# The last pair's denominators inside its value products, and the router's product between output products

## The chip, the cores and the metric

The kernel runs on one core of one Trainium2 chip. Its time is the device time of one execution in microseconds; before the change it is 2727.31 us, the median of 3 runs (2726.57 to 2728.21).

## The reference

Four layers act in turn on x of shape (4, 512, 64, 64), all float32. What bears on the change is the first layer and how it hands over to the second. Cut to that:

```python
# layer 0: attention over the 4096 positions of an image, 64 channels
t = jnp.einsum('oc,bchw->bohw', w_qkv, x)            # key, query, value
scores = jnp.einsum('bdk,bdq->bkq', key_, query)
attn = jax.nn.softmax(scores, axis=1)                # over the keys k
out = jnp.einsum('bdk,bkq->bdq', value, attn)
out = jnp.einsum('oc,bchw->bohw', w_out, out)
x = scale * out + x
# layer 1: a convolution whose weights are a mixture of 8 experts, one mixture for each image
pooled = x.mean(axis=(2, 3))
rw = jax.nn.sigmoid(pooled @ router_w.T + router_b)
W = jnp.einsum('be,eoihw->boihw', rw, experts)       # for each of w1 (1x1), w2 (3x3), w3 (1x1)
...
```

So the weights of layer 1 can't be mixed before the mean of layer 0's whole output is known. Layer 2 is a linear attention, layer 3 a projection with two cumulative sums and a gate.

## The kernel before

The images go one after another through the four layers. The 4096 positions of an image are eight blocks of 512, held as four pairs of 1024 (`NPAIR` is 4); a pair of x is one SBUF tile of 128 x 4 x 1024.

**Layer 0.** For each pair of query blocks and each of 32 tiles of 128 keys, `scores` makes the product s of keys and queries (TensorE, L248), its exponential into a ring of 12 buffers (ScalarE, L251), and adds it into acc (VectorE, L256). `values` (L263) multiplies the ring's buffer with the values into av. Step i of 128 is tile i mod 32 of pair i // 32. The steps go in groups of six: scores of a group, then values of the group before (the loop of L324); the last two steps have a group of their own. Softmax is taken without the subtraction of a maximum, so its denominators are the column sums of acc: `sums` makes them with a product by ones (den, L279), inverts them (rec, L282, VectorE), and multiplies av by them (o, L286 or L288). `out_product` (L302) then makes the layer's output y in four parts m of 128 channels, and `add_out` (L307) adds it to x.

For pairs 0 and 1 all of that is hung into later groups of the loop through the list `late`. The last two pairs, 2 and 3, are treated otherwise, since the router waits for them. Only their sums over positions are needed for the mean, and these follow from o by a small product: `o` leaves its sum in osum, and `prod` (L370) adds osum times a matrix of 128 x 8 to what the earlier pairs gave. The product with ones (logit, L372) sums it over partitions. L374 to L377 make the sigmoid as 1 / (1 + exp(-z)), the exponential on ScalarE (L375). `own`, `part` and `sel` (L379 to L385) lay the eight mixing coefficients out as small matrices, so that TensorE can mix the experts: `mix` (L187). Pieces 0 to 3 (ex_0) are the weights of layer 1's first product, pieces 4 to 9 (ex_4, ex_7) are mixed likewise; pieces 10 to 12 (ex_10) are mixed on VectorE by `mix_by_expert` (L177 and L179, eight steps into wc).

**The order at the end of layer 0.** TensorE's instructions stay in the order of the program text (`manual_schedule` over the whole). Before the change that is: the scores of steps 126 and 127, the values of steps 120 to 127, den of pair 3, four output products of pair 2 (which ScalarE evicts into ring buffers 8 to 11, L367), two of pair 3, logit, one of pair 3, the first mix, the last of pair 3, the two other mixes, and then layer 1's first product c (`conv1`, L433). VectorE has the order of the text inside the `with` block of L363; what stands outside of it, as the steps of `mix_by_expert`, the scheduler puts where it sees room.

**Buffers.** Products of 128 x 2 x 512 (s, y, c) share three PSUM buffers (`pair_psum`), so each such product waits until the one three back has been read. av, den, logit and mix take turns in two single banks (`bank`). Of SBUF, `bigp` has three large buffers and `xpool` five: ex_4 is loaded where the keys were, ex_10 where ring buffers 0 to 3 were, ex_7 where ring buffers 4 to 7 (ringx) were, each when its last reader is through.

Of the kernel before, what the change touches and what calls it, by code (L numbers as in the profile page):

```python
# [20 lines left out]
KC = C // P  # L21
# [3 lines left out]
NPAIR = NBLK // 2  # L25
# [20 lines left out]
def unshifted(ctx: ExitStack, tc: tile.TileContext, fits, x, wqkv_t, wout_t, router_t,  # L46
# [3 lines left out]
    nc = tc.nc  # L50
# [9 lines left out]
    def pair_psum(name):  # L60
        return ps.tile([P, 2, NB], F32, tag="s", name=name, bufs=3)

    def bank(name, shape=(P, NB)):
        return ps.tile(list(shape), F32, tag="acc", name=name)
# [4 lines left out]
    def block(name, shape=(P, NB)):  # L69
        return blkp.tile(list(shape), F32, tag="blk", name=name)  # L70

    def flat(t):
        return t.rearrange("p h n -> p (h n)")
# [24 lines left out]
    def col(i, n=1):  # L98
        return prm_sb[:, i:i + n]
# [36 lines left out]
    groups = [(0, 1, G1, B1, M1, V1), (1, 1, G2, B2, M2, V2), (2, KC, G3, B3, M3, V3)]  # L136
# [15 lines left out]
    def router_of_values():  # L152


        wo_t = pair_psum("wo_t")
        wot_sb = block("wot_sb")
        for kc in range(KC):
            nc.tensor.transpose(wo_t[:, 0, kc * P:(kc + 1) * P], wout_sb[:, kc * P:(kc + 1) * P], ident)
        nc.vector.tensor_copy(wot_sb, wo_t[:, 0, :])
        for kc in range(KC):  # L160
            nc.tensor.matmul(wo_t[:, 1, 0:E], wot_sb[:, kc * P:(kc + 1) * P], router_sb[:, kc, :],
                             start=kc == 0, stop=kc == KC - 1)
        nc.vector.tensor_scalar(wr_sb, wo_t[:, 1, 0:E], col(SCALE), 1.0 / HW, ALU.mult, ALU.mult)
# [27 lines left out]
    def layer0(b, xs):  # L191
# [20 lines left out]
        def v_transpose(pr, vv, vsb):  # L212
            tr = vv[:, 1, :].rearrange("p (j c) -> p j c", c=P)
            for j in range(TPB):
                nc.tensor.transpose(tr[:, j, :], vsb[:, j * P:(j + 1) * P], ident)
            t0 = pr * 2 * TPB
            nc.vector.tensor_copy(
                vt[:, t0:t0 + 2 * TPB, :].rearrange("p (h j) d -> p j h d", h=2),
                tr.rearrange("p j (h d) -> p j h d", h=2))
# [21 lines left out]
        accs, avs = {}, {}  # L241

        def scores(i):
            pr, kt = divmod(i, NT)
            s = pair_psum(f"s_{b}_{i}")
            for h in range(2):
                r = slice(h * D, (h + 1) * D)
                nc.tensor.matmul(s[:, h, :], key[r, kt * P:(kt + 1) * P],  # L248
                                 qry[r, pr * NB:(pr + 1) * NB], start=True, stop=True)
            p = ring[i % RING]  # L250
            nc.scalar.activation(p, s, AF.Exp)  # L251
            if kt == 1:
                accs[pr] = four(f"acc_{b}_{pr}")
                nc.vector.tensor_tensor(accs[pr], ring[(i - 1) % RING], p, ALU.add)
            elif kt > 1:
                nc.vector.tensor_tensor(accs[pr], accs[pr], p, ALU.add)  # L256

        def values(i):
            pr, kt = divmod(i, NT)
            if kt == 0:  # L260
                avs[pr] = bank(f"av_{b}_{pr}")
            for h in range(2):
                nc.tensor.matmul(avs[pr][h * D:(h + 1) * D, :], vt[:, kt, :], ring[i % RING][:, h, :],  # L263
                                 start=kt == 0, stop=kt == NT - 1)
            if kt < NT - 1:
                return None
            if pr < NPAIR - 1:
                av = block(f"avsb_{b}_{pr}")
                nc.scalar.copy(av, avs[pr])
                avs[pr] = av  # L270
            return pr

        recs, outs = {}, {}

        def sums(pr, early=True):
            av, acc = avs[pr], accs[pr]
            den = bank(f"den_{b}_{pr}")
            for h in range(2):
                nc.tensor.matmul(den[h * D:(h + 1) * D, :], ones[:, 0:D], acc[:, h, :],  # L279
                                 start=True, stop=True)  # L280
            rec = block(f"rec_{b}_{pr}")
            nc.vector.reciprocal(rec, den)  # L282
            o = block(f"o_{b}_{pr}")
            if pr >= NPAIR - 2:
                i = pr - NPAIR + 2
                nc.vector.scalar_tensor_tensor(o, av, 1.0, rec, ALU.mult, ALU.mult, accum_out=osum[:, i:i + 1])  # L286
            else:
                nc.vector.tensor_tensor(o, av, rec, ALU.mult)  # L288
            recs[pr], outs[pr] = rec, o
            if early:  # L290
                sum_range(pr)

        def sum_range(pr):
            i = b * NPAIR + pr
            nc.vector.tensor_reduce(stat[:, 0, i:i + 1], recs[pr], AX.X, ALU.add)
            nc.vector.tensor_reduce(stat[:, 1, i:i + 1], recs[pr], AX.X, ALU.min)

        def out_product(pr, m):
            y = pair_psum(f"y_{b}_{pr}_{m}")
            for h in range(2):  # L300
                r = slice(h * D, (h + 1) * D)
                nc.tensor.matmul(y[:, h, :], wout_sb[r, m * P:(m + 1) * P], outs[pr][r, :],  # L302
                                 start=True, stop=True)
            return y
# [6 lines left out]
        def out_step(pr, m):  # L311
            add_out(pr, m, out_product(pr, m))
# [9 lines left out]
        groups = [range(i, min(i + RING // 2, NPAIR * NT)) for i in range(0, NPAIR * NT, RING // 2)]  # L322
        late = []
        for g, group in enumerate(groups):  # L324
            for i in group:
                scores(i)
            if g == 0:
                v_transpose(*pend)
                if b == 0:
                    router_of_values()  # L330
                continue
            for _ in range(2):
                if late and late[0][0] < g:
                    late.pop(0)[1]()
            for i in groups[g - 1]:
                pr = values(i)
                if pr is not None:
                    late.append((g, lambda pr=pr: sums(pr)))
                    if pr < NPAIR - 2:
                        late += [(g + 1, lambda pr=pr, m=m: out_step(pr, m)) for m in range(KC)]  # L340
# [15 lines left out]
        pr = NPAIR - 1  # L356
# [5 lines left out]
        ex10 = load_experts(b, 10, 3, bigp, "big", pack=False)  # L362
        with tc.manual_schedule(engines={mybir.EngineType.DVE}):  # L363
            sums(pr, early=False)
            for m in range(KC):
                y = out_product(pr - 1, m)
                nc.scalar.activation(ring[8 + m], y, AF.Copy, scale=col(SCALE))  # L367
            ys = [out_product(pr, m) for m in range(2)]
            prod = small.tile([P, E], F32, tag="prod", name=f"prod_{b}")
            nc.vector.scalar_tensor_tensor(prod, wr_sb, osum[:, 1:2], base, ALU.mult, ALU.add)  # L370
            logit = bank(f"logit_{b}", (P, E))
            nc.tensor.matmul(logit, ones, prod, start=True, stop=True)  # L372
            rw = small.tile([P, E], F32, tag="rw", name=f"rw_{b}")
            nc.vector.tensor_tensor(rw, logit, col(RB, E), ALU.add)  # L374
            nc.scalar.activation(rw, rw, AF.Exp, scale=-1.0)  # L375
            nc.vector.tensor_scalar(rw, rw, 1.0, None, ALU.add)
            nc.vector.reciprocal(rw, rw)  # L377
            own = small.tile([P, 2, 4], F32, tag="own", name=f"own_{b}", bufs=1)
            nc.vector.tensor_tensor(own, rw.rearrange("p (g e) -> p g e", g=2),  # L379
                                    which[:, None, :].to_broadcast([P, 2, 4]), ALU.mult)  # L380
            part = small.tile([P, 2], F32, tag="part", name=f"part_{b}", bufs=1)
            nc.vector.tensor_reduce(part, own, AX.X, ALU.add)
            sel = small.tile([P, 2, 32], F32, tag="sel", name=f"sel_{b}", bufs=1)
            for g in range(2):
                nc.vector.tensor_scalar(sel[:, g, :], row, part[:, g:g + 1], None, ALU.mult)  # L385
            ys.append(out_product(pr, 2))
            add_out(pr, 0, ys[0])
            mix(wcq, sel, ex0)
            ys.append(out_product(pr, 3))
            for m in range(1, KC):  # L390
                add_out(pr, m, ys[m])
            for m in range(KC):
                xm = xs[pr - 1][:, m, :]
                nc.vector.tensor_tensor(xm, xm, flat(ring[8 + m]), ALU.add)
            sum_range(pr)
# [960 lines left out]
```

## Time and profile before

| Quantity | Value |
|---|---|
| time, median of 3 | 2727.31 us |
| span of the profiled execution | 2725.2 us |
| TensorE busy | 2668.1 us, 98% |
| VectorE busy | 1960.1 us, 72% |
| ScalarE busy | 1306.8 us, 48% |
| granted TensorE clock, mean | 0.997 |
| HBM traffic | 42 GB/s over the span |
| reciprocal rec of 128 x 512 | 3.35 us, 16 times |
| eviction of y by ScalarE (L367), 128 x 1024 | 1.115 us, 16 times |
| mixing step on VectorE (L179), 128 x 384 | 0.617 us, 28 times |

Busy times are unions of an engine's instructions; since matmuls overlap, a busy TensorE need not be at its peak. In the lines of groups and of the timeline, "out<-in" names tiles without their numbers, "xN" is how many instructions were merged, and a bracket gives the idle time of the engine before the instruction and what ended it. In the view of waits a line has who waited, for whom, the total in us, how often, and the longest.

### The profile page before, as it was taken

The numbers are of one execution on the slowest core, as the hardware profiler recorded it, in microseconds if no ns is written. First come the engines' busy times: TensorE is split into PE (matmuls) and PEld (weight loads), VectorE is DVE, ScalarE is ACT, GpSimd is POOL, SyncE is SP. The second block draws the span as 40 slices with busy tenths as digits, with TensorE's granted clock in tenths as the row PEclk, the third lists the DMA queues.
The fourth block names the chain that finished last, engine by engine and source line by source line (L and its number), as shares of the span: only waits on it lengthen the run. The fifth ranks groups of instructions, "written<-read, shape, count | busy, mean of one in ns | idle before, by whom it ended". The sixth has DMA issues, their size and how long they took to land.

```text
span 2725.2 us, 25637 instructions
## 1 busy us (share of the span) xinstructions
PE 2668.1 (98%) x10046; PEld 1112.3 (41%) x10046; DVE 1960.1 (72%) x2197; ACT 1306.8 (48%) x1483; POOL 10.8 (0%) x26
## 2 busy tenths in 40 slices
PE   8999999999999999999999999999999999999998
PEld 3333364344333345444433334544443333554443
DVE  2688766787468776678747777667874787866787
ACT  4545354445555535345555553525554545352545
POOL 1000000000000000000000000000000000000000
PEclk9999999999999999999999999999999999999999
DMA  5000210021200020002220002001121000200011
GB/s 188 1 1 0 101 31 1 16 108 76 80 1 1 1 101 31 1 24 100 77 78 1 1 1 101 32 0 62 62 113 42 1 1 4 98 31 1 31 46 48
DMA packets 34545, 115.15 MB, mean 42 GB/s; under 512 B 2928, under 2 KB 12144, under 8 KB 32880
## 3 DMA queue, kind: packets, MB, share of 16 engines
q1 hardware_dynamic: 34416, 113.43, 11.2%
q8 instruction: 81, 1.33, 0.2%
q14 instruction: 48, 0.39, 0.0%
HBM read 79.86 MB, written 33.55 MB: 42 GB/s over the span
## 4 chain that ended last, share of the span: by engine, by line
PE 86%; DVE 8%; ACT 3%; DMA 1%; issue 1%; SPq 1%; DVEq 0%; ACTq 0%
PE s L248 17%; PE av L263 17%; PE sx L758 14%; PE zy L758 11%; PE c L433 4%; PE kq L209 4%; PE c L482 3%; PE z L532 2%; PE c L505 2%; PE wv L676 2%; PE vv L209 2%; PE g L594 2%; PE xtr L577 2%; PE y L302 2%; PE c2e L482 2%
## 5 line engine op out<-in xcount | busy, mean ns | idle before, releaser
L248 PE MATMUL s<-qv,key 64*128 64x512 f32 x2048 | 468.9, 602 | 1.8 <-ACT ring L251 1.8
L256 DVE TENSOR_TENSOR acc<-acc,ring 128x1024 f32<-128x1024 f32 x312 | 381.7, 1223 | 101.0 <-ACT ring L251 72.0
L251 ACT ACTIVATE ring<-s 128x1024 f32<-128x1024 f32 x336 | 317.6, 1037 | 223.9 <-PE s L248 223.9
L263 PE MATMUL av<-ring,qv 128*64 128x512 f32 x1344 | 304.5, 595 | 0.0
L248 PEld LDWEIGHTS s<-qv,key 64*128 64x128 f32 x2048 | 188.9, 187 | 275.1 <-issue 172.1
L256 DVE TENSOR_TENSOR acc<-acc,ringx 128x1024 f32<-128x1024 f32 x168 | 205.5, 1223 | 101.7 <-ACT ringx L251 89.5
L251 ACT ACTIVATE ringx<-s 128x1024 f32<-128x1024 f32 x176 | 172.1, 1039 | 207.0 <-PE s L248 207.0
L758 PE MATMUL sx<-t,sx 128*128 128x512 f32 x512 | 236.8, 596 | 0.0
L263 PEld LDWEIGHTS av<-ring,qv 128*64 128x64 f32 x1344 | 93.2, 137 | 198.7 <-issue 198.7
L263 PE MATMUL av<-ringx,qv 128*64 128x512 f32 x704 | 167.1, 597 | 0.0
L763 ACT COPY zy<-sx 128x512 f32<-128x512 f32 x64 | 36.5, 570 | 240.1 <-PE sx L758 230.6
L808 DVE TENSOR_TENSOR_SCAN t<-sx,t 128x512 f32<-128x512 f32 x128 | 148.8, 1210 | 1.7
L758 PEld LDWEIGHTS sx<-t,sx 128*128 128x128 f32 x512 | 95.6, 190 | 128.0 <-issue 121.3
L797 ACT COPY t<-s 128x1024 f32<-128x1024 f32 x64 | 127.1, 1992 | 40.6 <-DVE s L791 40.6
L767 ACT ACTIVATE e<-sx,prm_sb 128x512 f32<-128x512 f32 x128 | 87.0, 686 | 123.8 <-PE sx L758 123.8
L791 DVE TENSOR_TENSOR_SCAN s<-wc,s 128x512 f32<-128x512 f32 x128 | 146.1, 1204 | 0.0
L814 ACT ACTIVATE s<-t 128x1024 f32<-128x1024 f32 x64 | 125.5, 1987 | 1.0 <-DVE t L808 0.9
L758 PE MATMUL sx<-t,wq 128*128 128x512 f32 x256 | 117.0, 597 | 7.5 <-ACT e L767 7.5
L209 PE MATMUL kq<-x,wqkv_sb 128*64 128x512 f32 x512 | 115.9, 605 | 7.2 <-DMA x<-in_x_dram 6.2
L758 PE MATMUL zy<-t,wq 128*128 128x512 f32 x256 | 118.6, 604 | 2.5 <-ACT zy L763 2.5
L758 PE MATMUL zy<-x,wq 128*128 128x512 f32 x256 | 116.2, 594 | 0.0
L758 PE MATMUL sx<-x,wq 128*128 128x512 f32 x256 | 116.1, 594 | 0.0
(195 smaller groups left out, 3388.5 us busy)
## 6 DMA issues: line engine op xcount, KB each, us to landing
out_dram<-s SPq DMA_DIRECT2D x64, 512.0 KB, 2.6
x<-in_x_dram SPq DMA_DIRECT2D x15, 2048.0 KB, 8.6
ex<-in_packed_dram SPq DMA_DIRECT2D x8, 1536.0 KB, 7.1
ex<-in_packed_dram SPq DMA_DIRECT2D x4, 2048.0 KB, 8.0
ex<-in_experts_dram SPq DMA_DIRECT2D x4, 2048.0 KB, 7.8
wq<-in_wproj_t_dram SPq DMA_DIRECT2D x32, 256.0 KB, 4.8
ex<-in_experts_dram SPq DMA_DIRECT2D x4, 1536.0 KB, 6.7
x<-in_x_dram SPq DMA_DIRECT2D x4, 512.0 KB, 6.8
```

What stands on the lines that cost most here:

```text
L209: nc.tensor.matmul(y[h * D:(h + 1) * D, :], wqkv_sb[:, kc, col0:col0 + D], xs[pr][:, kc, h * NB:(h + 1) * NB], start=kc == 0, stop=kc == K ...
L248: nc.tensor.matmul(s[:, h, :], key[r, kt * P:(kt + 1) * P], qry[r, pr * NB:(pr + 1) * NB], start=True, stop=True)
L251: nc.scalar.activation(p, s, AF.Exp)
L256: nc.vector.tensor_tensor(accs[pr], accs[pr], p, ALU.add)
L263: nc.tensor.matmul(avs[pr][h * D:(h + 1) * D, :], vt[:, kt, :], ring[i % RING][:, h, :], start=kt == 0, stop=kt == NT - 1)
L433: nc.tensor.matmul(y[:, h, :], wc[:, kc, :], xs[pr][:, kc, h * NB:(h + 1) * NB], start=kc == 0, stop=kc == KC - 1)
L482: nc.tensor.matmul(y[:, lo - a:hi - a], u, v[:, lo:hi], start=dy == 1, stop=dy == 2)
L758: nc.tensor.matmul(y, w[:, c, self.kind, self.j * P:(self.j + 1) * P], v[:, c, :], start=c == 0 and k in (1, 5), stop=c == 1, skip_group_c ...
L791: nc.vector.tensor_tensor_scan(self.half(i, h), along[:, self.j + 2 * i, :], self.half(i, h), 0.0, ALU.mult, ALU.add)
L797: nc.scalar.copy(self.t[i].rearrange("p (w r) -> p w r", w=W), self.s[i].rearrange("p (r w) -> p w r", w=W))
L808: nc.vector.tensor_tensor_scan(th, down[:, i, :], th, 0.0, ALU.mult, ALU.add)
L814: nc.scalar.activation(self.s[i].rearrange("p (r w) -> p w r", w=W), tw, AF.Sigmoid)
```

## The change

Two things are moved, in each of the four images; no operation is added or taken away.

- The denominators of the last pair: den and the reciprocal become a function of their own, `inverse_sums`. For the last pair it is called in the midst of the value products, ahead of step 124, when the scores of all 128 steps have been issued. `sums` then only multiplies av by the inverse.
- The router's product: of the four output products of pair 2, two stand ahead of `prod` and logit; the two others, and the first three of pair 3, stand behind `sel` in the text. Before, all four of pair 2 and two of pair 3 stood ahead of logit.

The aim is that the chain from the last values to the mixing coefficients has its long reciprocal beside the value products, and that TensorE has output products to make while the coefficients are worked out.

```diff
-        def sums(pr, early=True):
-            av, acc = avs[pr], accs[pr]
+        def inverse_sums(pr):
+            acc = accs[pr]
             den = bank(f"den_{b}_{pr}")
             for h in range(2):
                 nc.tensor.matmul(den[h * D:(h + 1) * D, :], ones[:, 0:D], acc[:, h, :],
                                  start=True, stop=True)
-            rec = block(f"rec_{b}_{pr}")
-            nc.vector.reciprocal(rec, den)
+            recs[pr] = block(f"rec_{b}_{pr}")
+            nc.vector.reciprocal(recs[pr], den)
+
+        def sums(pr, early=True):
+            if early:
+                inverse_sums(pr)
+            av, rec = avs[pr], recs[pr]
             o = block(f"o_{b}_{pr}")
...
-            for i in groups[g - 1]:
+            for n, i in enumerate(groups[g - 1]):
+                if g == len(groups) - 1 and n == 4:
+                    inverse_sums(NPAIR - 1)
                 pr = values(i)
...
             sums(pr, early=False)
-            for m in range(KC):
+            def out_before(m):
                 y = out_product(pr - 1, m)
                 nc.scalar.activation(ring[8 + m], y, AF.Copy, scale=col(SCALE))
-            ys = [out_product(pr, m) for m in range(2)]
+
+            for m in range(2):
+                out_before(m)
             prod = small.tile([P, E], F32, tag="prod", name=f"prod_{b}")
...
-            ys.append(out_product(pr, 2))
+            for m in range(2, KC):
+                out_before(m)
+            ys = [out_product(pr, m) for m in range(3)]
             add_out(pr, 0, ys[0])
             mix(wcq, sel, ex0)
             ys.append(out_product(pr, 3))
```

More of the change, by code (lines that the diff above doesn't have):

```diff
@@ L288, in sums @@
                 nc.vector.tensor_tensor(o, av, rec, ALU.mult)
-            recs[pr], outs[pr] = rec, o
+            outs[pr] = o
             if early:
```

## The prediction

> **What bounds the kernel now.** I read the page first: parts 1 and 4 say which engine sets the span.
>
> ```profile
> PE 2668.1 (98%) x10046; PEld 1112.3 (41%) x10046; DVE 1960.1 (72%) x2197; ACT 1306.8 (48%) x1483; POOL 10.8 (0%) x26
> ...
> PE 86%; DVE 8%; ACT 3%; DMA 1%; issue 1%; SPq 1%; DVEq 0%; ACTq 0%
> ```
>
> TensorE is busy nearly always, so only two things can shorten the span: fewer matmuls, or fewer moments in which TensorE stands. The change has the same matmuls, so I asked the view of waits for TensorE alone, and kept the two lines of the stretch that is edited:
>
> ```profile
> PE mix L187 <- DVE sel L385: 5.7, 4, 1.4
> ...
> PE y L302 <- ACT ring L367: 2.6, 4, 0.7
> ```
>
> Once per image TensorE stands 1.4 us before the first mix and 0.65 us before the second pair's worth of output products: 8.3 us of 2725. This is all that can be had. Third, the timeline of image 0 around that stretch, engine by engine (start, length, then what; a pair of matmul records is issued every 0.43 us, the lengths overlap):
>
> ```profile
> 291.51 3.65 PE L263 MATMUL av<-ring,qv 128*64 128x512 f32 x16
> 295.00 3.60 PE L263 MATMUL av<-ringx,qv 128*64 128x512 f32 x16
> 298.43 1.03 PE L279 MATMUL den<-acc,ones 128*64 128x512 f32 x4
> 299.39 3.70 PE L302 MATMUL y<-o,wout_sb 64*128 64x512 f32 x16
> 303.74 1.99 PE L302 MATMUL y<-o,wout_sb 64*128 64x512 f32 x8 [0.65 <-ACT ring L367]
> 305.66 0.39 PE L372 MATMUL logit<-prod,ones 128*128 128x8 f32 x2
> 305.98 1.13 PE L302 MATMUL y<-o,wout_sb 64*128 64x512 f32 x4
> 308.52 1.92 PE L187 MATMUL mix<-ex,sel 128*32 128x512 f32 x16 [1.41 <-DVE sel L385]
> 310.38 1.13 PE L302 MATMUL y<-o,wout_sb 64*128 64x512 f32 x4
> 311.43 2.79 PE L187 MATMUL mix<-ex,sel 128*32 128x384 f32 x32
> ```
>
> ```profile
> 291.83 2.55 DVE L256 TENSOR_TENSOR acc<-acc,ringx 128x1024 f32<-128x1024 f32 x2 [2.78 <-ACT ringx L251]
> ...
> 299.50 3.36 DVE L282 RECIPROCAL rec<-den 128x512 f32<-128x512 f32 x1 [5.12 <-PE den L279]
> ...
> 302.90 0.69 DVE L286 SCALAR_TENSOR_TENSOR o<-av,rec 128x512 f32<-128x512 f32 x1
> ...
> 303.63 0.23 DVE L370 SCALAR_TENSOR_TENSOR prod<-wr_sb,osum,base 128x8 f32<-128x8 f32 x1
> ...
> 306.09 0.17 DVE L374 TENSOR_TENSOR rw<-logit,prm_sb 128x8 f32<-128x8 f32 x1 [2.23 <-PE logit L372]
> 306.29 0.21 ACT L375 ACTIVATE rw<-rw 128x8 f32<-128x8 f32 x1 [1.59 <-DVE rw L374]
> ...
> 308.23 0.38 DVE L385 TENSOR_SCALAR sel<-row,part 128x32 f32<-128x32 f32 x2
> ...
> 308.52 4.86 DVE L307 SCALAR_TENSOR_TENSOR x<-y,prm_sb,x 128x1024 f32<-128x1024 f32 x4
> ```
>
> See two things. The sum of exponentials is complete at 294.38 (291.83 + 2.55), yet its product den runs at 298.43, behind all the value products; VectorE sits 5.12 us before the 3.36 us reciprocal. And the chain reciprocal, o, prod, logit, rw, sel, mix is serial, with logit queued behind two output products. In issue times TensorE loses a little more than the idle column says: the last pair of y issues at 302.50, so the next could at 302.92, and does at 303.74 (0.82); the product before the mix ends issuing at 306.94, the mix could at 307.04 and does at 308.52 (1.48). Together 2.30 us an image. The next layer's first matmul (c, L433) starts at 314.15. The stretch repeats in the other images within 0.1 us.
>
> [...] So whatever stands behind a waiting matmul waits with it, which the two stalls above show. [...] The exponential of the router will now stand between Copy evictions; the compiled program has no table load there, and in the trace the evictions (1.11 us long) start 1.00 us apart, an overlap of 0.11. [...] dependent wc steps of 0.62 us start 0.65 us apart.
>
> **Part 1: den and its reciprocal in the midst of the values.** It stands before the fifth of the last eight value steps, at 295.00, and takes 0.86 us there instead of at 298.43: same matmuls, same 128*64 shape, so no cost on TensorE. It adds a wait in front of four value steps: for the last acc, done at 294.38, 0.6 us early, in every image (2.87 us after the first of the eight steps, against 3.49). So nothing. The reciprocal starts when den has drained: 295.00 + 0.43 + 0.59 + 0.05 = 296.07, ends 299.43. It lies in VectorE's 5.12 us of idleness. The values now end where den ended, at 299.46. Hence o from 299.50 to 300.20 and prod to 300.47: 3.4 us earlier than before. One buffer, ringx, is read until 0.86 us later, so the load of ex_7 is issued at about 299.5 instead of 298.64; it took 8.9 us, lands at 308.4 and is needed by the third mix at 311: hidden.
>
> **Part 2: logit after two output products.** Output products start at 299.39 as before; two of them take until 301.21, a change of shape 0.13, logit 301.33 to 301.72 (its 0.32 us of TensorE is only moved). rw at 301.93. The exponential stands behind the second eviction on ScalarE, which starts at 301.57, so it starts one interval later, 302.57, and ends 302.78. Queued behind it are evictions three and four; the third starts at 302.82 instead of 302.57, the fourth ends at about 304.93. Before, sel started 1.74 us after the exponential's end (306.50 to 308.23), so it now starts at 304.51 and is complete at 304.90. TensorE meanwhile: six more products of 0.86 us and two changes of shape, 301.65 to 306.04; mix could start at 306.14. Their buffers: y needs its predecessor three back evicted, at 301.68, 302.68, 303.93, 304.93 for products due at 302.61, 303.47, 304.33, 305.19. All in time. So both old stalls, 2.30 us, vanish.
>
> **Part 3: what the order makes of it.** The compiled order of VectorE differs in one thing that the diff does not show: after sel, four of the mixing steps of wc (L179, of ex_10) now stand ahead of the first addition x<-y (L307), which used to follow sel at once. The steps are 0.65 us apart: 304.81 + 4 x 0.65 = 307.4, a little earlier for the overlap of the last, 307.30. The addition takes 1.28: 308.58. It frees the buffer that the fourth output product of the last pair needs, which stands behind the mix on TensorE: the mix takes 1.85 and would let it start at 307.99, so it waits until about 308.65. That is a new wait of 0.65 us, and everything behind it (second and third mix, layer 1) waits with it. From there to c it is 3.78 us as before: c at 312.4 instead of 314.15, a gain of 1.7 us.
>
> In image 0, ex_10 landed at 303.60, and the first wc step, which stands ahead of sel in VectorE's queue, would start at 303.34. So 0.3 is lost: 1.4. In the other images it landed 10.1 to 10.7 us after the first of the eight value steps against 11.8 needed.
>
> **Does it last?** The same wc steps are absent later, so VectorE has less to do in layer 1. ScalarE now makes the sums of taps ahead of the first h, and its second part waits for VectorE's taps, at about 320.7; h then ends at about 323.2, as before (323.26), and the taps are done. VectorE stood 1.80 us before the third pair's sums, waiting for h of TensorE's product: it is paced by TensorE and moves with it. c of layer 1 itself needs none of this: it ran 27.66 us without a gap. Later transfers are released by buffers that move too.
>
> Sum: 1.4 + 3 x 1.7 = 6.5 us; 2727.3 - 6.5 = 2720.8.
>
> **The rivals.** (B) The new wait is not there, because the steps of wc overlap more or the mix takes longer: 4 x 2.30 = 9.2, 2718.1. For it: the wait is only 0.65 us, the difference of two long sums. Against: the 0.65 us spacing is measured between dependent steps. (C) The chain to the first addition is later. It has no slack: each us is lost whole. If ex_10 lands 1 us later than I take it in every image, the gain is 0.7 to 0.9: some 3.3 us, 2724.0. For it: the landing spread from 10.1 to 12.1 us. Against: three of four were early by 1.1 us or more. (D) Slower: the taps ahead of h on ScalarE, or den waiting for acc, hold TensorE for longer than was gained, say 1.6 us net an image: 2727.3 + 6.4 = 2733.7. Against: layer 1's transformed products start at 341.89, while VectorE had the sums they need by 335.2, 6.7 us of room.
>
> **How the numbers follow.** My forecast 0.64, B 0.12, C 0.17, D 0.07. The bound of 0.2% is 5.45 us; the forecast of 6.5 lies only 1 us over it, so of its 0.64 I put 0.57 above; with B and a third of C, faster 0.75. The rest of the forecast and of C: same 0.19. Slower 0.06. The range takes in B at one end and C at the other: 2717.4 to 2724.0, outside of it D and the tails.
>
> **What would show it.** Right: TensorE's waits have no line of mix behind sel and none of y behind ring; y behind x of L307 appears, about 0.65 us, four times; den directly between two groups of av; rec's wait ends near 296.1; logit near 301.3; c starts 20.9 us after the first of the eight value steps, before 22.6. Wrong: a wait of av or den for acc; mix still waiting for sel; a wait of more than 1.5 us before the fourth product; a new gap before c of L482.

## The result, and the profile after

Of six runs each, the changed kernel takes 2718.76 us in the median (2717.71 to 2720.21) and the kernel before 2726.94 (2725.30 to 2728.21). The ratio is 0.9970, its 95% interval 0.9957 to 0.9983: faster by 8.2 us, and by 4.6 to 11.7 at the ends of the interval. The forecast was 6.5 us faster (2720.8), inside that interval. The span of the profiled execution went from 2725.2 to 2717.1 us at the same mean granted clock, 0.997. Line numbers from here on are those of the changed kernel; the numbers that moved and matter are y L307 (302 before), addition L312 (307), logit L381 (372), sel L394 (385), c L444 (433). L405 is the additions of pair 2, whose products were evicted to the ring.

The page of the kernel after, parts 1 and 4, engine shares:

```profile
PE 2667.3 (98%) x10046; PEld 1114.7 (41%) x10046; DVE 1961.2 (72%) x2197; ACT 1306.6 (48%) x1483; POOL 10.7 (0%) x26
...
PE 86%; DVE 9%; ACT 2%; DMA 1%; issue 1%; SPq 1%; DVEq 0%; ACTq 0%
```

The same matmuls keep TensorE busy for as long as before, to within 1 us; the bound is unchanged. The gain has to be in waits. The view of waits for TensorE alone, after (who waited, for whom, us in total, times, longest):

```profile
PE zy L769 <- ACT zy L774: 2.5, 4, 0.7
PE y L307 <- DVE x L312: 2.4, 4, 0.6
PE s L248 <- ACT ring L251: 1.8, 8, 0.2
```

The two lines of before, mix behind sel (5.7 us) and y behind ring (2.6), are not in the list at all. (What held y in the second of them was not the ring; see the experiment den_early_only.) One has come: y behind the addition x, four times 0.6. The neighbours are shown because they stand for what has not changed. In this view TensorE has 8.3 us less of the old and 2.4 us more of the new, 5.9 net; in issue times, as the forecast counts, it is more, as the offsets below show. TensorE's timeline of image 0, after (start, length, engine, line, what, how many; brackets as before):

```profile
291.49 3.65 PE L263 MATMUL av<-ring,qv 128*64 128x512 f32 x16
294.98 1.03 PE L279 MATMUL den<-acc,ones 128*64 128x512 f32 x4
295.84 3.60 PE L263 MATMUL av<-ringx,qv 128*64 128x512 f32 x16
299.37 1.99 PE L307 MATMUL y<-o,wout_sb 64*128 64x512 f32 x8
301.29 0.39 PE L381 MATMUL logit<-prod,ones 128*128 128x8 f32 x2
301.61 4.56 PE L307 MATMUL y<-o,wout_sb 64*128 64x512 f32 x20
306.10 1.93 PE L187 MATMUL mix<-ex,sel 128*32 128x512 f32 x16
308.62 1.13 PE L307 MATMUL y<-o,wout_sb 64*128 64x512 f32 x4 [0.60 <-DVE x L312]
309.68 2.79 PE L187 MATMUL mix<-ex,sel 128*32 128x384 f32 x32
312.40 4.13 PE L444 MATMUL c<-x,wc 128*128 128x512 f32 x9
```

From 291.49 to 306.10 there is no bracket: den, logit and five output products run one behind the other. The one bracket left is 0.60 us, before the fourth product of the last pair. VectorE's timeline of the same stretch says why:

```profile
291.81 2.56 DVE L256 TENSOR_TENSOR acc<-acc,ringx 128x1024 f32<-128x1024 f32 x2 [2.78 <-ACT ringx L251]
296.06 3.36 DVE L282 RECIPROCAL rec<-den 128x512 f32<-128x512 f32 x1 [1.69 <-PE den L279]
299.52 0.69 DVE L291 SCALAR_TENSOR_TENSOR o<-av,rec 128x512 f32<-128x512 f32 x1
...
304.50 0.38 DVE L394 TENSOR_SCALAR sel<-row,part 128x32 f32<-128x32 f32 x2
304.80 2.58 DVE L179 SCALAR_TENSOR_TENSOR wc<-ex,rw,wc 128x384 f32<-128x384 f32 x4
307.29 1.28 DVE L312 SCALAR_TENSOR_TENSOR x<-y,prm_sb,x 128x1024 f32<-128x1024 f32 x1
```

The reciprocal starts at 296.06 and ends at 299.42, 0.10 us before o needs it: it is as long as before, but now runs beside the value products. Behind sel stand the four mixing steps, and only then, at 307.29, the first addition; it ends at 308.57, and the fourth product starts 0.05 later.

To compare kernels I measured, in every image, when each operation starts after the first of the last eight value steps (291.49 above). These are differences of timeline entries, image 0, in us; "last y" is the fourth output product of the last pair:

| kernel | den | rec | logit | sel | first mix | first addition | last y | c |
|---|---|---|---|---|---|---|---|---|
| before | 6.92 | 7.99 | 14.15 | 16.72 | 17.01 | 17.01 | 18.87 | 22.64 |
| after | 3.48 | 4.56 | 9.79 | 13.01 | 14.60 | 15.79 | 17.12 | 20.90 |
| den_early_only | 3.48 | 4.56 | 13.29 | 15.86 | 16.15 | 16.15 | 18.00 | 21.78 |
| router_early_only | 6.92 | 7.99 | 12.49 | 15.03 | 18.97 | 18.47 | 20.83 | 24.60 |
| den_two_steps_earlier | 2.92 | 4.05 | 11.00 | 14.22 | 15.81 | 17.00 | 18.33 | 22.11 |
| add_before_mixing | 3.48 | 4.56 | 9.79 | 12.14 | 14.60 | 13.01 | 16.46 | 20.23 |

c after is 20.90 in all four images and was 22.64: 1.74 us an image, 6.96 in all. That is the part of the 8.2 us whose cause is in sight. The other 1.1 us of the spans is smaller than the spread of runs of one kernel (2.5 us among the six above), and no stretch shows it in all four images: some 0.75 us of it lie in layer 2, where TensorE waits on work that VectorE has behind the landing of the weights wq (image 3 gains 1.0 us there, image 1 loses 0.7), and 0.4 between the end of layer 2 of image 2 and layer 0 of image 3.

### The profile page after: what moved, and what is told of

The parts are those of the page before. It is cut to its first block, busy times and chain, and to the rows that moved or that the text cites. A ratio compares the mean times of both kernels' runs of the same rounds, so it can differ in the third digit from the quotient of the medians.

```text
span 2717.1 us, 25649 instructions
## 1 busy us (share of the span) xinstructions
PE 2667.3 (98%) x10046; PEld 1114.7 (41%) x10046; DVE 1961.2 (72%) x2197; ACT 1306.6 (48%) x1483; POOL 10.7 (0%) x26
## 4 chain that ended last, share of the span: by engine, by line
PE 86%; DVE 9%; ACT 2%; DMA 1%; issue 1%; SPq 1%; DVEq 0%; ACTq 0%
PE s L248 17%; PE av L263 17%; PE sx L769 14%; PE zy L769 11%; PE c L444 4%; PE kq L209 4%; PE c L493 3%; PE c L516 2%; PE z L543 2%; PE wv L687 2%; PE vv L209 2%; PE g L605 2%; PE xtr L588 2%; PE c2e L493 2%; PE y L307 1%
```

## The experiments

Theory: each half of the change does one thing. The early denominators take the reciprocal off the serial chain; the early logit lets output products fill the time of the sigmoid. The early logit is of no use alone, since it waits for the reciprocal unless that is early too; the early denominators alone leave the wait of the mix as it was. What is not gained is the 0.6 us of the new wait, and its cause is the order of VectorE, not the number of its instructions. The rival: one half gives all of it, and the other is idle. Each kernel is compared with the kernel before on the same chip (medians 2726.33 us for the first four, 2726.03 for the last four).

**The change once more (again).** No edit.

> The changed kernel unaltered, a second profile. Theory (two old stalls of 2.30 us an image removed, one new wait of 0.6 us): layer 1's first product c starts 20.90 us after the first of the last eight value steps in all four images, to 0.05 us; the 1.1 us by which the first profile gained more than 4 x 1.74 us is the landing of the projection weights wq in layer 2, which varies from 9.1 to 10.2 us after the last transformed product from one execution to the next, so its sum over the images will differ again and the time will be 2717.7 to 2720.2. Rival (the change itself makes layer 2 shorter): the sum of the landings stays 0.7 us or more under that of before.

2718.85 us (2716.44 to 2720.68), ratio 0.9971 (0.9959 to 0.9983): 7.5 us faster. c came 20.90 us after the first value step, 20.93 in image 1; the new wait is 2.4 us in all again. So the gain is 8.2 and 7.5 us in the two measurements, of which 7.0 lie in the stretch. Of the theory on the rest, one half held: it is not the change. The addition sx, which waits for the landing of wq, starts 41.22 us after the last transformed product of layer 1 in the kernel before, added over the images, 40.47 in the first profile of the changed kernel and 40.98 here, so the rival's 0.7 us did not come back. But the landing is not the whole of the rest either: here 1.2 us of it lie ahead of the stretch of image 0 (the first value step at 290.34 instead of 291.51), in work that the change does not touch.

**Denominators early, logit where it was (den_early_only).**

```diff
-            for m in range(2):
+            for m in range(KC):
                 out_before(m)
+            ys = [out_product(pr, m) for m in range(2)]
...
-            for m in range(2, KC):
-                out_before(m)
-            ys = [out_product(pr, m) for m in range(3)]
+            ys.append(out_product(pr, 2))
```

> Only the denominators and the reciprocal of the last pair are moved; logit stands behind six output products, as before. Theory (one serial chain; each part needs the other): the wait of y goes, logit at 13.3 us after the first of the last eight value steps, sel 2.9 later, the wait of mix for sel stays at 1.4 us of idle TensorE; c at 21.75, against 22.64 before: 0.9 us an image, 3.6 in all, 2723.3. Rival 1 (the early reciprocal is the whole gain): c at 20.9, 2719. Rival 2 (it gives nothing alone): 2727.

2722.60 us, ratio 0.9985 (0.9979 to 0.9992): 3.7 faster, by the table 4 x (22.64 - 21.78) = 3.4. The waits of TensorE in this kernel:

```profile
PE kq L209 <- DMA x<-in_x_dram: 5.9, 1, 5.9
PE mix L187 <- DVE sel L395: 5.7, 4, 1.4
PE xtr L587 <- ACT pos L551: 4.3, 4, 1.1
```

Mix waits for sel for exactly as long as before the change, 5.7 us: that wait goes only when logit is moved as well. The early reciprocal alone removes the other, which the view of before put down to the ring. Here six output products run without a gap:

```profile
298.84 5.48 PE L307 MATMUL y<-o,wout_sb 64*128 64x512 f32 x24
```

The fifth, the first of the last pair, starts at 302.38, when the second eviction into the ring has ended (302.14) but the third has not (303.14); so it needs only the second. In the kernel before, the second ended at 302.68, and the fifth product came only at 303.74. It multiplies o of the last pair, which was complete at 303.60; that the third eviction ended at 303.69, close by, is why the view names the ring. What ended last was o, and o waits for the reciprocal.

**Logit early, denominators where they were (router_early_only).**

```diff
             for n, i in enumerate(groups[g - 1]):
-                if g == len(groups) - 1 and n == 4:
-                    inverse_sums(NPAIR - 1)
...
+            inverse_sums(pr)
             sums(pr, early=False)
```

> Only the router's product is moved; den and its reciprocal stand behind all value products, as before. Theory: logit waits for prod at 12.4 us after the first of the last eight value steps, while output products due at 9.8 stand behind it, so TensorE stands 2.6 us there; the wait for sel goes; VectorE has five steps of wc ahead of the first addition, so the last output product waits 0.7 us; c at 23.6, against 22.64 before: 1.0 us an image lost, 4 in all, 2731. Rival (the order of the router's product is a gain by itself, the 1.4 us of the mix): c at 21.2, 2721.

2734.22 us, ratio 1.0027 (1.0016 to 1.0038): 7.9 slower, and slower than expected. TensorE's timeline of image 0:

```profile
299.54 1.99 PE L307 MATMUL y<-o,wout_sb 64*128 64x512 f32 x8
304.16 0.36 PE L380 MATMUL logit<-prod,ones 128*128 128x8 f32 x2 [2.63 <-DVE prod L378]
304.45 6.26 PE L307 MATMUL y<-o,wout_sb 64*128 64x512 f32 x20
310.64 1.92 PE L187 MATMUL mix<-ex,sel 128*32 128x512 f32 x16
```

The 2.63 us wait is what the theory asks for: the queue stands behind logit, logit behind prod, prod behind the reciprocal. What was not expected is the line below. The same twenty matmuls took 4.56 us after the change and take 6.26 here, with no bracket. The view of windows of this kernel has the granted clock (the columns after the window and its length are the busy times of PE, PEld, DVE, ACT and POOL, then PEclk, DMA share, GB/s):

```profile
302.00:304.00 2.00, 0.00 (x0) 0.00 (x0) 1.93 (x4) 0.84 (x1) 0.00 (x0) 1.00 0.83 307
304.00:306.00 2.00, 1.84 (x8) 1.13 (x10) 1.11 (x6) 0.34 (x2) 0.00 (x0) 0.81 0.75 320
306.00:308.00 2.00, 2.00 (x6) 0.68 (x4) 1.96 (x7) 1.41 (x2) 0.00 (x0) 0.50 0.05 18
308.00:310.00 2.00, 2.00 (x10) 0.93 (x8) 1.90 (x4) 0.69 (x1) 0.00 (x0) 0.83 0.00 0
```

After the wait the clock is halved for a while: from 306 to 308 it is 0.50, and six matmul records of y fall there; the kernel after has twelve of them in two microseconds (304 to 306). The forecast of c was 23.6; it came at 24.60. The slow clock cost 1.70 us (6.26 against 4.56), but spared the last y its wait for x, which the forecast had at 0.7 us: the slowed queue came to that product after the addition was done. In image 3 the mix came 20.38 us after the first value step rather than 18.97, and c 26.01. So the wait of 2.63 us cost TensorE more than its length; den_first and router_after_three follow this up.

**The first addition ahead of the mixing steps (add_before_mixing).** The steps of `mix_by_expert` are written inside the fixed order, behind the additions of three of the four products.

```diff
-            for m in range(1, KC):
+            for m in range(1, KC - 1):
                 add_out(pr, m, ys[m])
+            mix_by_expert(wcq, rw, ex10)
+            add_out(pr, KC - 1, ys[KC - 1])
...
-        mix_by_expert(wc, rw, ex10)
```

> Both parts of the change, and the eight mixing steps of wc on VectorE fixed behind three of the four additions, so that the first addition follows sel at once. Theory (the new wait is the buffer of the last output product, held until the first addition): the wait of y for x goes, no other takes its place, c at 20.30 us after the first of the last eight value steps, 0.6 us an image and 2.4 in all faster than the changed kernel: 2716.4. Rival (another wait stands right behind, in the mixes or in layer 1, as the taps come later on VectorE): c at 20.9 or a new gap before layer 1's transformed products, 2718.8.

2717.91 us (2715.55 to 2718.78), ratio 0.9966 (0.9952 to 0.9980). VectorE of image 0, which begins 0.95 us earlier in this execution:

```profile
302.68 0.39 DVE L394 TENSOR_SCALAR sel<-row,part 128x32 f32<-128x32 f32 x2
303.54 3.67 DVE L312 SCALAR_TENSOR_TENSOR x<-y,prm_sb,x 128x1024 f32<-128x1024 f32 x3 [0.47 <-PE y L307]
307.12 0.60 DVE L177 TENSOR_SCALAR wc<-ex,rw 128x384 f32<-128x384 f32 x1
```

The addition now follows sel, the wait of y for x is gone from TensorE's list, and c comes at 20.23: 0.67 us an image, as expected (20.30). That shows the cause of the new wait. Over the whole kernel 2.7 us should follow; the median is 0.9 us under that of the change run beside it and the intervals overlap, so the gain is shown in the stretch, not in the time. In these two profiles layer 2 takes 0.9 us of it back, between the last transformed product and the transposes ktr (87.5 us over the images against 86.6); see the last experiment.

**Denominators two value steps earlier (den_two_steps_earlier).**

```diff
-                if g == len(groups) - 1 and n == 4:
+                if g == len(groups) - 1 and n == 2:
```

> The changed kernel with den and the reciprocal ahead of step 122 instead of 124. Theory (the place has 0.6 us of slack before acc is complete): den is due 1.72 us after the first of the last eight value steps and acc is complete at 2.9, so TensorE stands 1.2 us there, which nothing repays, since o waits for the last value step anyway; c at 22.1 instead of 20.90, 1.2 us an image and 4.8 in all slower than the changed kernel, 2723.6; the granted clock stays at 1.00, as with the 1.4 us stalls of before. Rival (a waiting den costs nothing, value steps are worked meanwhile): c at 20.9.

2723.84 us, ratio 0.9992 (0.9985 to 0.9998): 2.2 faster than the kernel before, and 5.0 slower than the changed kernel (4.8 expected). TensorE of image 0:

```profile
290.67 1.94 PE L263 MATMUL av<-ring,qv 128*64 128x512 f32 x8
293.60 1.08 PE L279 MATMUL den<-acc,ones 128*64 128x512 f32 x4 [0.99 <-DVE acc L256]
294.51 1.89 PE L263 MATMUL av<-ring,qv 128*64 128x512 f32 x8
```

Den is due two value steps, 1.7 us, earlier than in the change, but it starts only 0.56 us earlier (2.92 in place of 3.48), since acc is complete no sooner. TensorE is idle for 0.99 us, and six value steps stand behind it. Those 0.56 us are the slack of the forecast, measured from the other side. c is at 22.11, 1.21 us later, so the rival (a waiting den costs nothing) falls.

**Denominators ahead of all the last values (den_first).** As the last, with `n == 0`, four value steps ahead of where the change has it.

> The changed kernel with den and the reciprocal ahead of the first of the eight value steps. TensorE stands about 2.85 us in one piece. Theory A (a stall of 2.6 us or more lowers the granted clock to a half for some microseconds, as in the run with the router's product alone moved): granted clock 0.5 within the 5 us behind the stall, value steps spaced 0.85 us instead of 0.43 for a while, c at 25.4 or later, 2737 or more. Theory B (that slowness came from the output products themselves or the transfers beside them): clock 1.00, c at 23.8, 2730.5.

2734.76 us, ratio 1.0030 (1.0017 to 1.0042): 8.7 slower. TensorE waits for acc 11.4 us in all, 2.85 an image, and in three of four images the clock is halved behind it. The time lies between the forecasts of theory A (2737 or more) and theory B (2730.5). Two windows of image 0; the stall ends at 294.56, inside the first:

```profile
293.00:295.00 2.00, 0.44 (x2) 0.20 (x4) 1.41 (x2) 0.00 (x0) 0.00 (x0) 1.00 0.76 301
295.00:297.00 2.00, 2.00 (x8) 0.72 (x6) 0.82 (x1) 0.00 (x0) 0.00 (x0) 0.50 0.96 412
```

The clock of 0.50 came here behind a stall at another place, ahead of value products, so it is not made by the output products. Nor is it made by the transfers beside it: in image 1 a stall of the same 2.85 us was followed by a clock of 1.00, while as much was moved (418 GB/s from 973 to 975 us, 412 above). So the length of the stall alone does not decide.

**Logit behind three output products (router_after_three).** The edit of router_early_only, with `range(3)` and `range(3, KC)`: a shorter stall, 1.77 us.

> Denominators late, as before, and the router's product behind three output products, not two. The stall before logit shortens from 2.63 to 1.8 us. Theory A (only a stall of 2.6 us or more lowers the clock): granted clock 1.00, mix at 16.4 us and c at 22.0 after the first of the last eight value steps, 0.6 us an image faster than before, 2724. Theory B (any output product behind the wait is slow): c at 23.7, 2730.5.

2730.06 us, ratio 1.0013 (1.0004 to 1.0022), 4.0 slower. Two images of this kernel, 0 and 2, TensorE's timeline of each:

```profile
303.96 0.36 PE L380 MATMUL logit<-prod,ones 128*128 128x8 f32 x2 [1.77 <-DVE prod L378]
304.25 5.40 PE L307 MATMUL y<-o,wout_sb 64*128 64x512 f32 x16
...
1654.39 0.36 PE L380 MATMUL logit<-prod,ones 128*128 128x8 f32 x2 [1.77 <-DVE prod L378]
1654.68 3.70 PE L307 MATMUL y<-o,wout_sb 64*128 64x512 f32 x16
```

The stall is the same to 0.01 us, and the sixteen matmuls behind it take 5.40 and 3.70 us. In three of four images the clock fell behind the stall of 1.77 us (image 0: 0.50 from 306 to 308; image 2: 1.00 from 1654 to 1662); c came 23.75 us after the first value step where the clock fell and 22.05 where it did not, ahead of the 22.64 of before. The extra 1.70 us is the halved clock, and it alone turns this order from a gain into a loss. Theory A, a bound on the stall near 2.6 us (the 2.63 of router_early_only), falls with images 0, 1 and 3. Theory B, that output products behind a wait are slow in themselves, falls with image 2, and so does any bound by length alone.

**The sums of layer 2's weights after the last of layer 1 (sums_of_weights_later).** add_before_mixing, and in addition one stretch of layer 2 whose order on VectorE is kept as written. The scheduler had put an addition of loaded weights (sx from wq, L709) far ahead of its place in the text, and VectorE stood before it. VectorE of image 0, add_before_mixing:

```profile
384.05 0.42 DVE L504 SCALAR_TENSOR_TENSOR yy<-sp 128x256 f32<-128x256 f32 x1
393.23 1.22 DVE L709 TENSOR_TENSOR sx<-wq 128x1024 f32<-128x1024 f32 x1 [8.76 <-DMA wq<-in_wproj_t_dram]
394.37 1.28 DVE L519 SCALAR_TENSOR_TENSOR x<-c,bn_s,x 128x1024 f32<-128x1024 f32 x1
```

```diff
-        products(0, ahead(1))
-        weights[2]()
+        with tc.manual_schedule(engines={mybir.EngineType.DVE}):
+            products(0, ahead(1))
+            weights[2]()
```

> The kernel with the first addition ahead of the mixing, and in layer 2 the four sums of the projection weights on VectorE fixed behind the copies of products(0) instead of where the scheduler put them. Theory (the 8.8 us that VectorE waits for the landing of wq holds up the additions queued behind, and passes the landing's variation on to TensorE): VectorE no longer waits for wq, the transposes ktr start at the same time after the last transformed product in all four images, TensorE's waits of xtr for pos and x and of c for x in layer 2 (1.9 us an image) shrink or go, 1.3 to 2.4 us an image, 2708 to 2713. Rival (the wait is hidden behind TensorE's own products, the variation comes from elsewhere): 2716 to 2719, ktr varies as before.

2711.72 us (2710.78 to 2713.72), ratio 0.9948 (0.9933 to 0.9962). The same stretch of VectorE:

```profile
383.31 0.42 DVE L504 SCALAR_TENSOR_TENSOR yy<-sp 128x256 f32<-128x256 f32 x1
391.23 1.28 DVE L519 SCALAR_TENSOR_TENSOR x<-c,bn_s,x 128x1024 f32<-128x1024 f32 x1 [7.50 <-PE c L517]
392.43 0.68 DVE L555 TENSOR_SCALAR sp<-sp 128x1024 f32<-128x1024 f32 x1
```

VectorE stands nearly as long, but for TensorE's own product, and what it did behind the load (the activations of layer 1's result, which the transposes of layer 2 need) is no longer late. The time from the last transformed product of layer 1 to the transposes of layer 2 is 21.03 us in all four images, although wq landed 9.93, 10.32, 9.48 and 10.31 us after that product; in add_before_mixing it came to 0.3 to 0.7 us more, and the later the sum of wq started, the more. This version is 14.3 us under the kernel before, and all its five runs are under every run of the changed kernel: it beats both. Of the 6.1 us between its span (2709.9) and that of add_before_mixing (2716.0), the view of waits has 3.6 in two lines: the transposes xtr behind pos fall from 4.4 to 1.5, and c behind x (0.7) goes. By the starts of the operations, which count a stall more fully than the idle column, 4.8 us of the 6.1 lie between the last transformed product and the second group of transposes xtr, 1.2 us an image; 0.7 lie ahead of the edited part of image 0 and 0.6 behind layer 2, in work that both kernels share.

## Why the prediction was right

**Part 1, den in the midst of the values: held.** Forecast 295.00, measured 294.98, with acc complete at 294.37 and no wait; rec at 296.07, measured 296.06; o at 299.50, measured 299.52. den_two_steps_earlier shows the 0.6 us of slack in acc to be real.

**Part 2, logit between output products: held.** Logit at 301.33, measured 301.29. The exponential did come behind the second eviction, at 302.56 (302.57 forecast), sel at 304.50 (304.51), mix at 306.10 (306.14). Both old stalls are gone. For the second, part 2 showed only that the buffers are in time, as if the ring had been the hold, which is how the view of before labels it; what had held the product was o, and it is part 1 that moved o, by 3.4 us. The forecast had both, so nothing came of it. The text counted six products between logit and mix; the trace has five (twenty matmuls), and the time that it gave, to 306.04, was that of five.

**Part 3, the new wait: held in place and size.** Addition at 307.29 (307.30), last product at 308.62 (308.65), c at 312.40 (312.4). In issue times, as the forecast counts, the product could have started at 307.95 (306.10 + 1.85), so it waited 0.67 us against the 0.65 forecast; the idle column shows 0.60 of it. add_before_mixing shows that it is VectorE's order that makes it: with the addition first, the wait goes and c comes 0.67 us earlier.

**The mis-sized term: image 0.** The sum had 1.4 for it, 0.3 less than the others, for the landing of ex_10. That took a landing of one execution (12.1 us after the first value step) for a property of image 0. In the kernel after, ex_10 landed there at 10.1 us, the first mixing step ran at 303.33, ahead of sel and without a wait, and image 0 gained the same 1.74 as the rest. So 4 x 1.74 = 6.96 in place of 6.5. That no image lost anything was in part luck: in images 1 and 2 the landing came at 11.5 and 11.4 us, and the step needs it at 11.83. **"Does it last?" held:** the wait of c L516 behind x, the nearest candidate for a new gap, is 0.4 us in all, 0.6 before; c L493, which the text named, has none. The second part of the taps came at 320.49 (320.7), and h ended at 322.83 (323.2). The spans differ by 1.1 us more than the stretch; in the second profile that rest lies elsewhere (again), so it is not the change's.

**The rivals.** B (no new wait, 2718.1) is nearest in time, but the trace speaks against it: the wait is there, four times 0.6. As an order of its own it exists, as add_before_mixing, at 2717.91. C asked for an ex_10 that lands later and for a chain without slack. Its mechanism shows once, and small: in image 1 of again ex_10 landed at 11.83 us, the first mixing step started 0.03 us late, and c came 0.03 us late (20.93). A landing of 12.1 us, as in image 0 of before, would by the same reckoning have cost that image 0.3 us. D asked for a wait of den for acc or of layer 1's work; in this kernel there is none. den_first shows that D was near: den four value steps earlier makes it 2734.76.

**What neither forecast nor rivals had.** The two halves are not a sum: 3.7 us faster and 7.9 slower each by itself, 7.5 faster together. Alone, the early logit is put in front of the reciprocal it depends on. The forecast was right because it walked through both halves in one timeline.

## What to carry to other kernels

Before moving a product ahead on an engine that keeps its order, find what it waits for and move that first: here the one half gave about half of the gain alone, and the other was harmful alone. Then read the compiled order of the helping engine behind the move, since four small steps set ahead of one addition cost 0.6 us an image, and one operation set ahead of its load held back a later stage by 1.2 us an image. When a view names what ended a wait, check it against the operands: one that ended 0.1 us away can be named in its place. Count a stall on TensorE at possibly more than its length: behind one of 1.77 us the granted clock fell to 0.50 in three of four images, and sixteen products took 5.40 us in place of 3.70 (last section).

## What was not expected of the hardware

**The granted clock fell behind some stalls and not behind others of the same length.** Stalls of TensorE, and the granted clock (PEclk) that the view of windows gives from about their end on, in stretches of 2 us:

| kernel, image | stall | next product at | from, to | granted clock |
|---|---|---|---|---|
| before, 0 (wo_t L161) | 3.19 | 63.08 | 62 to 70 | 0.65, 0.50, 0.50, 0.65 |
| after, 0 (wo_t L161) | 3.19 | 62.92 | 62 to 70 | 0.68, 0.50, 0.50, 0.61 |
| den_first, 0 | 2.85 | 294.56 | 294 to 300 | 0.75, 0.50, 0.89 |
| den_first, 1 | 2.85 | 972.03 | 971 to 979 | 1.00, 1.00, 1.00, 1.00 |
| router_early_only, 0 | 2.63 | 304.16 | 304 to 310 | 0.81, 0.50, 0.83 |
| router_early_only, 3 | 2.63 | 2333.24 | 2333 to 2341 | 0.50, 0.50, 0.50, 0.85 |
| router_after_three, 0 | 1.77 | 303.96 | 304 to 310 | 0.75, 0.50, 0.90 |
| router_after_three, 2 | 1.77 | 1654.39 | 1654 to 1662 | 1.00, 1.00, 1.00, 1.00 |
| before, 0 (mix) | 1.41 | 308.52 | 308 to 314 | 1.00, 1.00, 1.00 |

The first two rows are of a wait that every kernel here has (wo_t L161 behind wot_sb, 3.2 us at about 60 us), outside of the edited stretch. At 2.85 us and at 1.77 us the same stall has a low clock behind it in one image and 1.00 in another; what decides between them was not shown. Where the clock fell, the sixteen products of router_after_three took 1.70 us longer (5.40 against 3.70), and the twenty of router_early_only 1.70 us in image 0 (6.26 against the 4.56 of the changed kernel) and 2.90 in image 3 (7.46).
